# Slot sums of a gathered attention as accumulating float32 transposes, on one Trainium2 core

## The chip, the cores and the metric

The kernel runs on one core of a Trainium2 chip. The metric is device microseconds of one execution; the kernel before has a median of 3311.32 us over three runs (3306.66 to 3313.20). The profile is of one further execution, whose own time was 2781.14 us and whose span in the trace is 2779.3 us. The measured runs are thus 530 us longer than the profiled one, and all rows below come from the profiled one.

Engines: PE is the matrix engine (PEld its weight loads), DVE the vector engine, ACT the scalar engine, POOL the engine that here issues the gathers, SP the one that issues plain loads.

## The reference, cut to what matters

A graph network with four layers over 3327 nodes, each with 256 features. About 0.48% of the adjacency matrix is set, some 16 neighbours per node.

```python
x = ...      # (3327, 256) float32
adj = ...    # (3327, 3327) int32, Bernoulli(0.0048)

# layer 0: one attention score per row, projection, layer norm
h = x @ Wt.T + bt
s = leaky_relu(h @ Wa.T + ba)
w = softmax(where(adj > 0, s, NEG), axis=1)
x = layer_norm(x + (w @ h) @ Wp.T + bp)

# layers 1, 2, 3: multi-head attention over the neighbours, then a feed-forward
for L in (1, 2, 3):
    q, k, v = split(layer_norm(x) @ w_qkv)            # 8 heads of 32
    scores = where(adj != 0, q . k * SCALE, -inf)
    out = softmax(scores) @ v                         # (3327, 256)
    x = x + out @ w_proj + b_proj
    x = x + gelu(layer_norm(x) @ w1 + b1) @ w2 + b2
```

## The kernel before

The kernel makes a list of neighbours for every node, sorts the nodes by number of neighbours, and puts them into 26 blocks of 128. A block b has `CAPS[b]` slots (40 for the fullest, 10 for the emptiest, 448 in all): slot s of node p holds its s-th neighbour. In each layer POOL gathers, for each slot of a block, 128 rows of 512 float32 numbers (key and value), four slots to a buffer, ten buffers in a ring.

DVE multiplies keys with the query and sums per head, ACT takes the exponential, DVE multiplies the values with the weights into `vw` (128 nodes x 4 slots x 256). What is left is the sum over slots, for which PE is used:

```python
def values(self, b, s0):
    ...
    if s0 == 0:
        while len(self.po) > 1:
            self.short.pop(0)()
        self.po[b] = ps_o.tile([P, 512], FP, tag="o", ...)        # one PSUM bank, two of them
    ...
    vw = work.tile([P, GS * D], FP, tag="vw", bufs=3, ...)
    nc.vector.tensor_mul(vw..., v, self.wp[b]...)                  # L1361
    for s in range(0, n, 2):
        m = min(2, n - s) * D
        nc.tensor.matmul(self.po[b][:, :m], ident, vw[:, s * D:s * D + m],   # L1366
                         start=(s0 + s == 0), stop=(s0 + s + 2 >= S), skip_group_check=True)
    self.issue()                                                   # the next gathers of the ring
    if s0 + GS >= S:
        self.short += self.block(b)
```

`ident` is the identity, so a product only copies `vw` into PSUM and adds. Two slots go into one product, so the even and odd slots are summed apart, 256 columns each. The end of a block folds the two, turns the sum (nodes on partitions) into its transpose (features on partitions), which the projection needs as stationary operand, and projects:

```python
def copy():      c["o"] = ...; nc.scalar.copy(c["o"], self.po[b][:, :D])             # L1384
def fold():      nc.vector.tensor_add(c["o"], c["o"], self.po[b][:, D:])             # L1387
def turn():      # two 128x128 transposes back into po                               # L1391
def copy_T():    c["oT"] = ...; nc.scalar.copy(c["oT"], self.po[b][:, :2 * P])       # L1396
def project():   # bias (L1400), then oT @ w_proj into po[:, D:]                     # L1402
def add():       # x += po[:, D:] (L1406), statistics; at the end of a chunk of four blocks
                 # its feed-forward steps are put on the list self.long
return [lambda: None, copy, lambda: None, fold, turn, copy_T, project, lambda: None, add]
```

These short steps are taken one or two at a time between the groups of the blocks that follow, and so are the long steps of a chunk: feed-forward up (L1445) and down (L1468), and the queries, keys and values of the next layer (L1498). Layer 3 has no next layer; it scatters rows of the output instead (L1511).

Ahead of the layers lies a front end that reads the adjacency matrix, makes the lists, and does layer 0. There each group of four blocks counts how many nodes have which number of neighbours. PE adds one-hot rows into `places`, and DVE reads the result:

```python
def soft(self):
    ...
    nc.vector.tensor_tensor(OH[...], num..., top..., ALU.is_equal)          # L892
    at = places[...]
    for j in range(n): ...                                                  # L903
        nc.tensor.matmul(at[:, j, :], lhsT, OH[:, m, :], start=False, stop=True, ...)
    t = aw.tile([P, 4, nd], FP, tag="place", bufs=1, ...)
    nc.vector.tensor_mul(t, at[:, :n, :], OH[:, b0:b0 + n, :])              # L906
    nc.vector.tensor_reduce(rank[:, b0:b0 + n], t, AX.X, ALU.add)           # L907
    if b0 + n == NB:
        ...                                                                 # L909
    # ... small vector work, then two exponentials on ACT
def mix(self): ...                     # the step after: weights times sums
```

Each engine runs its instructions in the order in which the program states them.

Of the kernel before, what the change touches and what calls it, by code (L numbers as in the profile page):

```python
# [8 lines left out]
FP = mybir.dt.float32  # L9
# [3 lines left out]
ALU = mybir.AluOpType  # L13
AX = mybir.AxisListType
# [3 lines left out]
P = 128  # L18
N = 3327
D = 256  # L20
# [12 lines left out]
NB = (N + P - 1) // P  # L33
# [490 lines left out]
def sparse_path(ctx, tc, ins, out, dram, flag):  # L524
    nc = tc.nc
# [97 lines left out]
    with tc.tile_pool(name="a", bufs=1) as a, tc.tile_pool(name="aw", bufs=2) as aw, \  # L623
# [44 lines left out]
        o = 0  # L668
# [172 lines left out]
        class Group:  # L841
# [36 lines left out]
            def soft(self):  # L878


                g, n, b0 = self.g, self.n, self.blocks[0]

                def sv(name):
                    t = aw.tile([P, 4], FP, tag="s_" + name, bufs=1, name=f"s_{name}_{g}")
                    return t[:, :n]

                sg = S.s[:, b0:b0 + n]
                dg = deg[:, b0:b0 + n]
                nc.vector.tensor_copy(dg, self.acc[:, :n, H0])
                top = sv("top")  # L890
                nc.vector.tensor_scalar(top, dg, float(LMAX), None, ALU.min)
                nc.vector.tensor_tensor(OH[:, b0:b0 + n, :],  # L892
                                        num[:, None, :nd].to_broadcast([P, n, nd]),
                                        top[:, :, None].to_broadcast([P, n, nd]), ALU.is_equal)

                at = places[:, :4 * nd].rearrange("p (b k) -> p b k", k=nd)
                for j in range(n):
                    i = b0 + j
                    add = [(tri, i)] + [(ones_bf, k) for k in range(b0, i)]
                    if g:  # L900
                        add += [(rest_tri, i - 4)] + [(ones_bf, k) for k in range(i - 3, b0)]
                    for lhsT, m in add:
                        nc.tensor.matmul(at[:, j, :], lhsT, OH[:, m, :], start=False, stop=True,  # L903
                                         skip_group_check=True)
                t = aw.tile([P, 4, nd], FP, tag="place", bufs=1, name=f"place_{g}")[:, :n]
                nc.vector.tensor_mul(t, at[:, :n, :], OH[:, b0:b0 + n, :])  # L906
                nc.vector.tensor_reduce(rank[:, b0:b0 + n], t, AX.X, ALU.add)  # L907
                if b0 + n == NB:
                    nc.tensor.matmul(at[:, n - 1, :], rest_tri, OH[:, NB - 1, :], start=False,  # L909
                                     stop=True, skip_group_check=True)  # L910
                    S.all = at[:, n - 1, :]
                non, ga, fa, m1, m0, tt, mx = (
                    sv(k) for k in ("non", "ga", "fa", "m1", "m0", "tt", "mx"))
                nc.vector.tensor_scalar(non, dg, -1.0, float(N), ALU.mult, ALU.add)
                nc.vector.tensor_scalar(ga, dg, 0.0, None, ALU.is_gt)
                nc.vector.tensor_scalar(fa, non, 0.0, None, ALU.is_gt)
                nc.vector.tensor_scalar(tt, ga, -NEG0, NEG0, ALU.mult, ALU.add)
                nc.vector.tensor_mul(m1, sg, ga)
                nc.vector.tensor_add(m1, m1, tt)
                nc.vector.tensor_scalar(tt, fa, -1.0, 1.0, ALU.mult, ALU.add)  # L920
                nc.vector.tensor_mul(m0, sg, tt)
                nc.vector.scalar_tensor_tensor(m0, fa, NEG0, m0, ALU.mult, ALU.add)
                nc.vector.tensor_max(mx, m1, m0)
                nc.vector.tensor_sub(m1, m1, mx)
                nc.vector.tensor_sub(m0, m0, mx)
                nc.scalar.activation(m1, m1, AF.Exp)
                nc.scalar.activation(m0, m0, AF.Exp)
                self.non, self.m1, self.m0, self.tt = non, m1, m0, tt

            def mix(self):  # L930
                g, n, b0, acc = self.g, self.n, self.blocks[0], self.acc
                m1, m0, tt = self.m1, self.m0, self.tt
                z = aw.tile([P, 4], FP, tag="s_z", bufs=1, name=f"s_z_{g}")[:, :n]
                nc.vector.tensor_mul(z, deg[:, b0:b0 + n], m1)
                nc.vector.tensor_mul(tt, self.non, m0)
                nc.vector.tensor_add(z, z, tt)
                nc.vector.reciprocal(z, z)
                nc.vector.tensor_mul(m1, m1, z)
                nc.vector.tensor_mul(m0, m0, z)
                shape = [P, n, H0]  # L940
                nb = self.nb = aw.tile([P, 4, H0], FP, tag="nb", bufs=1, name=f"s_nb_{g}")[:, :n]
                t3 = aw.tile([P, 4, H0], FP, tag="t3", bufs=1, name=f"s_t3_{g}")[:, :n]
                nc.vector.tensor_sub(t3, S.hsum[:, None, :].to_broadcast(shape), acc[:, :n, :H0])
                nc.vector.tensor_mul(t3, t3, m0[:, :, None].to_broadcast(shape))
                nc.vector.tensor_mul(nb, acc[:, :n, :H0], m1[:, :, None].to_broadcast(shape))
                nc.vector.tensor_add(nb, nb, t3)

            def project(self):
                g, n = self.g, self.n
# [322 lines left out]
    class Layer:  # L1272
# [77 lines left out]
        def values(self, b, s0):  # L1350

            L, S = self.L, CAPS[b]
            n = min(GS, S - s0)
            t = self.tiles.pop((b, s0))
# [3 lines that stand above are left out]
                self.po[b] = ps_o.tile([P, 512], FP, tag="o", name=f"po_{L}_{b}")  # L1358
            v = t[:, :n, D:2 * D].rearrange("p s (h d) -> p s h d", d=HD)
            vw = work.tile([P, GS * D], FP, tag="vw", bufs=3, name=f"vw_{L}_{b}_{s0}")  # L1360
            nc.vector.tensor_mul(  # L1361
                vw[:, :n * D].rearrange("p (s h d) -> p s h d", h=HEADS, d=HD), v,
                self.wp[b][:, s0:s0 + n, :, None].to_broadcast([P, n, HEADS, HD]))
            for s in range(0, n, 2):
                m = min(2, n - s) * D
                nc.tensor.matmul(self.po[b][:, :m], ident, vw[:, s * D:s * D + m],  # L1366
                                 start=(s0 + s == 0), stop=(s0 + s + 2 >= S),
                                 skip_group_check=True)
            self.issue()
            if s0 + GS >= S:  # L1370
                self.short += self.block(b)


        def block(self, b):
            L, w, c = self.L, self.w, {}
            x = t2[:, b, :D]
            chunk = CHUNK[b]
            if b == chunk[0]:
                self.n2 = Norm(len(chunk), f"f{L}_{b}")
            n2 = self.n2  # L1380

            def copy():
                c["o"] = work.tile([P, D], FP, tag="o", name=f"o_{L}_{b}")
                nc.scalar.copy(c["o"], self.po[b][:, :D])  # L1384

            def fold():
                nc.vector.tensor_add(c["o"], c["o"], self.po[b][:, D:])  # L1387

            def turn():
                for k in range(2):  # L1390
                    nc.tensor.transpose(self.po[b][:, k * P:(k + 1) * P],  # L1391
                                        c["o"][:, k * P:(k + 1) * P], ident)

            def copy_T():
                c["oT"] = work.tile([P, 2 * P], FP, tag="oT", name=f"oT_{L}_{b}")
                nc.scalar.copy(c["oT"], self.po[b][:, :2 * P])  # L1396

            def project():
                ps = self.po[b][:, D:]
                nc.tensor.matmul(ps, ones_bf[:96, :], bias3[:, 0, :], start=True, stop=False)  # L1400
                for k in range(2):
                    nc.tensor.matmul(ps, c["oT"][:, k * P:(k + 1) * P], w["w_proj"][:, k, :],  # L1402
                                     start=False, stop=(k == 1))

            def add():
                nc.vector.tensor_add(x, x, self.po.pop(b)[:, D:])  # L1406
                n2.stats(chunk.index(b), x)
                if b == chunk[-1]:
                    self.long += self.chunk(chunk, n2)
                    at = ORDER.index(b) + 1  # L1410
                    turns = sum(len(slots[i]) for i in ORDER[at:at + CB])
                    turns = 5 if at == NB - 1 else turns - 2
                    self.rate = sum(cost for cost, _ in self.long) / max(turns, 1)

            return [lambda: None, copy, lambda: None, fold, turn, copy_T, project, lambda: None, add]

        def chunk(self, blocks, n2):
            L, w, nxt = self.L, self.w, self.nxt
# [221 lines left out]
```

## Time and profile before

| what | value |
|---|---|
| measured time, median of 3 | 3311.32 us |
| profiled execution, span | 2779.3 us |
| PE busy | 1952.0 us, 70% |
| DVE busy | 1961.9 us, 71% |
| ACT busy | 806.5 us, 29% |
| POOL busy | 1361.8 us, 49% |
| moved by DMA | 453.66 MB, mean 163 GB/s |
| granted PE clock, mean | 0.836 of full |

How to read it: a busy share is an average over the whole span. A row of a group of instructions gives its line, engine and operation, what it writes and reads, its shapes and count, then busy us and mean ns of one, then the idle time of its engine just before it, and what ended most of that. A line of the list of waits gives who waited for whom, the total in us, how many times, and the longest. Slices are fortieths of the span, 69.5 us each, in tenths of busy time. Busy times of PE overlap where matmuls are pipelined, so the spacing of their starts says more than their mean duration. A float32 product shows as two PE records.

### The profile page before, as it was taken

To read this page: it belongs to the slowest core of one execution; us is meant where nothing else is said; L and a number is where in the kernel's file an instruction comes from. 1 tells how busy PE (TensorE), PEld (TensorE's weight loads), DVE (VectorE), ACT (ScalarE), POOL (GpSimd) and SP (SyncE) were. 2 spreads that over 40 slices of the span, in tenths; PEclk is the share of its full clock that TensorE was granted. 3 is DMA by queue.
4 is the path that set the end of the run, shared out by engine and by line. 5 is a ranking of instruction groups with operands and counts; after the bars stand their busy time and mean duration, and the time that the engine had idled before them with its cause. 6 is when DMAs were issued, how large, how long until landed. Compare 5 with 4: busy or idle time off the path is not lost. (4 is left out here: it accounts for less than half of the span.)

```text
span 2779.3 us, 21889 instructions
## 1 busy us (share of the span) xinstructions
PE 1952.0 (70%) x6409; PEld 1045.3 (38%) x6409; DVE 1961.9 (71%) x4061; ACT 806.5 (29%) x1398; POOL 1361.8 (49%) x1458
## 2 busy tenths in 40 slices
PE   5657665248788887884377887887853678867866
PEld 4546553114333333442133443433431333333334
DVE  6597888577877777733788677778427878778852
ACT  5346552102332322321022332232320222222221
POOL 4000000377766666601776565566017777776741
PEclk9768776678899898897788898898976898988988
DMA  6224420677766666613776565566227766666650
GB/s 235 99 106 154 155 81 32 198 217 217 222 196 200 202 182 186 182 34 100 209 211 201 168 195 180 158 190 178 50 70 210 210 183 199 201 190 184 198 130 15
DMA packets 144478, 453.66 MB, mean 163 GB/s; under 512 B 29521, under 2 KB 40156, under 8 KB 141021
## 3 DMA queue, kind: packets, MB, share of 16 engines
q0 software_dynamic: 113056, 370.26, 46.0%
q1 hardware_dynamic: 9834, 53.90, 5.5%
q10 hardware_dynamic: 21458, 28.02, 2.9%
q8 instruction: 52, 0.85, 0.1%
q14 instruction: 78, 0.64, 0.1%
HBM read 420.64 MB, written 31.42 MB: 163 GB/s over the span
## 5 line engine op out<-in xcount | busy, mean ns | idle before, releaser
L1298 POOL DMA_INDIRECT kv<-kv,t x1344 | 1272.8, 947 | 810.0 <-issue 350.4
L1366 PE MATMUL po<-vw,s_ident 128*128 128x512 f32 (+1 forms) x1380 | 770.4, 694 | 497.4 <-DVE vw L1361 447.6
L1320 DVE TENSOR_TENSOR kv<-kv,q 128x1024 f32<-128x1024 f32 (+3 forms) x363 | 413.3, 1139 | 312.6 <-ACT q L1306 156.5
L1366 PEld LDWEIGHTS po<-vw,s_ident 128*128 128x128 f32 x1380 | 285.3, 220 | 846.5 <-issue 468.3
L1321 DVE TENSOR_REDUCE sc<-kv 128x32 f32<-128x1024 f32 (+3 forms) x363 | 414.1, 1141 | 12.4
L1361 DVE TENSOR_TENSOR vw<-kv,w 128x1024 f32<-128x1024 f32 x333 | 371.3, 1127 | 0.2
L1445 PE MATMUL pu<-fT,s_w 128*128 128x512 f32 (+3 forms) x768 | 308.1, 536 | 1.0 <-ACT fT L596 1.0
L1468 PE MATMUL py<-gT,s_w 128*128 128x512 f32 (+2 forms) x672 | 283.4, 549 | 0.0
L1451 ACT ACTIVATE gT<-pu,pvb 128x512 f32<-128x512 f32 (+3 forms) x192 | 116.4, 607 | 361.0 <-PE pu L1445 360.7
L1445 PEld LDWEIGHTS pu<-fT,s_w 128*128 128x128 f32 x768 | 150.6, 206 | 140.5 <-issue 116.0
L711 POOL MEMSET s_abf<- 128x1 bf16 x23 | 2.2, 105 | 375.2 <-DVE s_v L731 248.3
L1468 PEld LDWEIGHTS py<-gT,s_w 128*128 128x128 f32 x672 | 127.6, 191 | 122.0 <-issue 104.4
L723 PE MATMUL s_ptb<-s_ident_bf,s_abf 128*128 128x128 bf16 x676 | 69.8, 273 | 77.3 <-ACT s_abf L714 64.0
L735 DVE MAX8 cand<-s_v 128x8 f32<-128x208 bf16 x416 | 118.0, 359 | 0.9
L588 ACT ACTIVATE xn_f<-t,nm_f,rqy_f 128x256 f32<-128x256 f32 x78 | 42.9, 593 | 247.5 <-DVE nm_f L582 240.1
L1498 PE MATMUL pk<-s_w_qkv,nT 128*128 128x512 f32 x208 | 104.4, 626 | 8.9 <-ACT nT L596 8.9
L1335 ACT ACTIVATE sc<-sc,mx 128x120 f32<-128x120 f32 (+6 forms) x78 | 32.0, 410 | 259.8 <-DVE mx L1332 259.2
L1406 DVE TENSOR_TENSOR t<-t,po 128x256 f32<-128x256 f32 x78 | 32.5, 417 | 103.8 <-PE po L1402 97.9
L1486 DVE TENSOR_TENSOR t<-t,pd 128x256 f32<-128x256 f32 x75 | 29.5, 408 | 91.0 <-PE pd L1482 91.0
L723 PEld LDWEIGHTS <-s_abf 128*128 128x128 bf16 x676 | 58.8, 125 | 91.8 <-ACT s_abf L714 70.8
L855 PE MATMUL s_pa<-s_aT,s_hs 128*128 128x256 bf16 x338 | 80.4, 286 | 13.2 <-DVE s_hs L817 13.2
L724 ACT COPY s_aT<-s_ptb 128x896 bf16<-128x896 bf16 x104 | 82.7, 859 | 19.9 <-PE s_ptb L723 19.7
(292 smaller groups left out, 2343.5 us busy)
## 6 DMA issues: line engine op xcount, KB each, us to landing
s_a<-in_adj_dram SPq DMA_DIRECT2D x25, 1663.5 KB
kv<-kv,t POOLq DMA_INDIRECT x1344, 3.7
kv<-kvr ACTq DMA_DIRECT2D x52, 256.0 KB
kv<-s_kvr ACTq DMA_DIRECT2D x26, 256.0 KB
s_w<-in_L_gnn_w_dram SPq DMA_DIRECT2D x6, 1024.0 KB
t<-ql ACTq DMA_DIRECT2D x6, 592.0 KB
t<-s_x ACTq DMA_DIRECT2D x6, 512.0 KB
s_w_qkv<-in_L_gnn_w_qkv_dram SPq DMA_DIRECT2D x3, 768.0 KB
```

The source lines that it names most:

```text
L723: nc.tensor.transpose(pt[:, m, :], self.abf[:, k * P:(k + 1) * P], ident_bf)
L724: nc.scalar.copy(aT[:, k0:k0 + len(ks), :], pt[:, :len(ks), :])
L735: nc.vector.max(out=self.cand[:, s, :], in_=self.v[:, s, :])
L1298: nc.gpsimd.indirect_dma_start(out=t[:, s, :], out_offset=None, in_=kv[L], in_offset=bass.IndirectOffsetOnAxis(ap=t2[:, b, k:k + 1].bitcas ...
L1320: nc.vector.tensor_mul(k, k, self.q[b][:, None, :].to_broadcast([P, n, D]))
L1321: nc.vector.tensor_reduce(self.sc[b][:, s0:s0 + n, :], k.rearrange("p s (h d) -> p s h d", d=HD), AX.X, ALU.add)
L1361: nc.vector.tensor_mul(vw[:, :n * D].rearrange("p (s h d) -> p s h d", h=HEADS, d=HD), v, self.wp[b][:, s0:s0 + n, :, None].to_broadcast([ ...
L1366: nc.tensor.matmul(self.po[b][:, :m], ident, vw[:, s * D:s * D + m], start=(s0 + s == 0), stop=(s0 + s + 2 >= S), skip_group_check=True)
L1445: nc.tensor.matmul(c["pu", f][:, :n], w["w1"][:, e, f * P:(f + 1) * P], c["hT"][:, e, :n], start=(e == 0), stop=(e == 1))
L1451: nc.scalar.activation(g[:, :n], c.pop(("pu", f))[:, :n], AF.Gelu_apprx_tanh, bias=w["b1"][:, f:f + 1])
L1468: nc.tensor.matmul(c["py"][e][:, :n], w["w2"][:, f, e * P:(e + 1) * P], g[:, :n], start=(f == 0), stop=last)
L1498: nc.tensor.matmul(ps[:, :c1 - c0], c["hT"][:, e, j * P:(j + 1) * P], nxt["w_qkv"][:, e, c0:c1], start=(e == 0), stop=(e == 1))
```

## The change

The product with the identity becomes a transpose that accumulates in PSUM. For each slot PE takes the two halves of `vw` (128 nodes x 128 features) as stationary operand and passes the identity through in transpose mode; the result, 128 features x 128 nodes, is added to what PSUM holds. So the sum over slots comes out transposed as the projection wants it, even and odd slots are not kept apart, and the end of a block needs no copy, fold and turn. The aim is to spare PE the arithmetic of the float32 products, and the other engines the steps at the end of a block.

Apart from that, the front end's reading of `places` moves from `soft` to the end of `mix`, one step of its plan later, so that DVE need not stand and wait for PE there.

```diff
-                t = aw.tile([P, 4, nd], FP, tag="place", bufs=1, name=f"place_{g}")[:, :n]
-                nc.vector.tensor_mul(t, at[:, :n, :], OH[:, b0:b0 + n, :])
-                nc.vector.tensor_reduce(rank[:, b0:b0 + n], t, AX.X, ALU.add)
-                if b0 + n == NB: ...            # (cut: moved along unchanged)
+            def place(self):
+                g, n, b0 = self.g, self.n, self.blocks[0]
+                at = places[:, :4 * nd].rearrange("p (b k) -> p b k", k=nd)
+                t = aw.tile([P, 4, nd], FP, tag="place", bufs=1, name=f"place_{g}")[:, :n]
+                nc.vector.tensor_mul(t, at[:, :n, :], OH[:, b0:b0 + n, :])
+                nc.vector.tensor_reduce(rank[:, b0:b0 + n], t, AX.X, ALU.add)
+                if b0 + n == NB: ...
@@ mix
                 nc.vector.tensor_add(nb, nb, t3)
+                self.place()
@@ values
-            for s in range(0, n, 2):
-                m = min(2, n - s) * D
-                nc.tensor.matmul(self.po[b][:, :m], ident, vw[:, s * D:s * D + m],
-                                 start=(s0 + s == 0), stop=(s0 + s + 2 >= S),
-                                 skip_group_check=True)
+            for s in range(n):
+                for k in range(2):
+                    at = s * D + k * P
+                    nc.tensor.matmul(self.po[b][:, k * P:(k + 1) * P], vw[:, at:at + P], ident,
+                                     is_transpose=True, start=(s0 + s == 0 and k == 0),
+                                     stop=(s0 + s + 1 == S), skip_group_check=True)
@@ block
-            def copy(): ...
-            def fold(): ...
-            def turn(): ...
-            return [lambda: None, copy, lambda: None, fold, turn, copy_T, project, lambda: None, add]
+            return [lambda: None, copy_T, project, lambda: None, add]
```

More of the change, by code (lines that the diff above doesn't have):

```diff
@@ L904, in soft @@
                                          skip_group_check=True)
-                t = aw.tile([P, 4, nd], FP, tag="place", bufs=1, name=f"place_{g}")[:, :n]
-                nc.vector.tensor_mul(t, at[:, :n, :], OH[:, b0:b0 + n, :])
-                nc.vector.tensor_reduce(rank[:, b0:b0 + n], t, AX.X, ALU.add)
[L908 to L911, printed above, removed]
                 non, ga, fa, m1, m0, tt, mx = (
@@ L928, in soft @@
                 self.non, self.m1, self.m0, self.tt = non, m1, m0, tt
+            def place(self):
[4 more added lines that the diff above has]
+                nc.vector.tensor_reduce(rank[:, b0:b0 + n], t, AX.X, ALU.add)
+                if b0 + n == NB:
+                    nc.tensor.matmul(at[:, n - 1, :], rest_tri, OH[:, NB - 1, :], start=False,
+                                     stop=True, skip_group_check=True)
+                    S.all = at[:, n - 1, :]
             def mix(self):
@@ L1380, in block @@
             n2 = self.n2
[L1382 to L1392, printed above, removed]
             def copy_T():
```

## The prediction

> **What bounds the kernel now.** I read the page's first two parts, then its costliest groups, then busy time in 30 us stretches, then the waits, and last the chain of work that ended last.
>
> Page, busy shares and the 40 slices:
>
> ```profile
> PE 1952.0 (70%) x6409; PEld 1045.3 (38%) x6409; DVE 1961.9 (71%) x4061; ACT 806.5 (29%) x1398; POOL 1361.8 (49%) x1458
> ...
> PE   5657665248788887884377887887853678867866
> DVE  6597888577877777733788677778427878778852
> ...
> POOL 4000000377766666601776565566017777776741
> PEclk9768776678899898897788898898976898988988
> ```
>
> No engine is full. POOL separates five parts: a front end without gathers (to 521 us, the first gather), and three layers of gathers, each followed by a tail in which POOL is at 0 or 1 (the next layer cannot gather before the last row of keys and values is written).
>
> Costliest groups:
>
> ```profile
> L1298 POOL DMA_INDIRECT kv<-kv,t x1344 | 1272.8, 947 | 810.0 <-issue 350.4
> L1366 PE MATMUL po<-vw,s_ident 128*128 128x512 f32 (+1 forms) x1380 | 770.4, 694 | 497.4 <-DVE vw L1361 447.6
> L1320 DVE TENSOR_TENSOR kv<-kv,q 128x1024 f32<-128x1024 f32 (+3 forms) x363 | 413.3, 1139 | 312.6 <-ACT q L1306 156.5
> ```
>
> The slot sums are PE's largest item, 770 of 1952 us. POOL's timeline shows 0.30 us between gathers of 0.95 us: one per 1.25 us at best. Layer 1 issues 473 POOL transfers between 521.1 and 1179.7 us (447 gathers of keys and values, 26 of rows): 473 x 1.25 = 591 of 659 us, so 67 us of stall. Layer 2: 448 in 649 us, 560, stall 89. Layer 3: 467 in 609 us (some are output rows), 584, stall 25. Together 181 us. The stalls come once per chunk of four blocks, about every 103 us in layers 1 and 2.
>
> Who is late when POOL stalls? Two short stretches of layer 1, then one whole period of layer 2 and a stretch of layer 3:
>
> ```profile
> core 0: us, PE busy (x) PEld busy (x) DVE busy (x) ACT busy (x) POOL busy (x), PEclk, DMA share, GB/s
> ...
> 950.00:980.00 30.00, 30.00 (x71) 13.73 (x70) 21.43 (x32) 10.72 (x21) 20.37 (x22) 0.92 0.68 195
> 1160.00:1190.00 30.00, 30.00 (x76) 13.73 (x76) 16.88 (x18) 9.63 (x22) 15.81 (x17) 1.00 0.72 165
> ...
> 1702.00:1804.00 102.00, 83.58 (x215) 39.29 (x214) 76.18 (x133) 30.62 (x52) 60.99 (x65) 0.88 0.59 175
> ...
> 2450.00:2540.00 90.00, 70.22 (x174) 31.99 (x173) 69.31 (x108) 22.43 (x35) 64.96 (x69) 0.89 0.66 196
> ```
>
> Columns: stretch, length, busy time of PE, PE weight loads, DVE, ACT, POOL, granted clock, DMA. PE is busy for the whole of the first two at nearly full clock, while DVE is at 71 and 56% and POOL issues 22 and 17 transfers where 24 would fit. A period of layer 2 holds 65 transfers, 81 us at POOL's best, but takes 102, with PE busy for 84 and DVE for 76. Layer 3 gets 69 into 90 us. It has the same slot sums but no projection of the next layer (line 1498, 104 + 53 us for two layers), and it stalls 25 us instead of 89. So PE is what makes layers 1 and 2 late, in bursts. DVE itself waits behind it; its list of waits in layer 1 begins:
>
> ```profile
> DVE kv L1320 <- ACT q L1306: 62.9, 14, 7.2
> DVE t L1406 <- PE po L1402: 33.4, 10, 6.5
> ```
>
> ACT is late there because its queue stands at a copy out of PSUM that PE has not filled (the waits list ACT for 117.5 us behind line 1366 and 124.4 behind line 1391, in all).
>
> **What the skill says.** "Perfetto Trace Analysis", in Optimizing Tensor Performance, Transposes: a transpose should be issued as one, since it skips the arithmetic. The chain that ended last has both side by side at one clock:
>
> ```profile
> 2709.93 0.45 PE pd L1482 x4
> ...
> 2713.01 3.62 PE po L1366 x4
> ...
> 2717.06 1.72 PE po L1366 x4
> ```
>
> Four float32 transposes take 0.45 us, 0.11 each; four passes of the slot product take 1.72, 0.43 each, or 3.62 at half clock. "FP8 and Floating Point Precision", TensorE Precision Notes, says a true float32 product needs four passes. The trace agrees: each product is two records, and each streams 512 columns in 0.43 us, 0.84 ns a column, against 0.11 us for 256 bf16 columns in line 855: four times as long in all. A float32 transpose is one record of 128 columns at the same 0.84 ns. "PSUM — Partial Sum Buffer", The four PSUM rules, says a float32 transpose sets the bits as a matmul does, so it should accumulate; no run here shows it yet. "TensorE: Matmul & The Clock Gate", Part 4, warns that transposes don't count as activity for the clock. This trace disagrees, for bf16: the 3.4 us from 105.1 us hold 26 transposes and no other matmul at a granted clock of 0.50, and the next 3.4 us have 0.99.
>
> **The change, part by part.**
>
> *Slot sums.* Four slots were two products of 512 columns, four records, 4 x 0.43 = 1.72 us at full clock. They become eight transposes, 8 x 0.11 = 0.88 us; each has its own weight load, but in the transposes of line 591 loads and passes overlap (starts 0.21 us apart at half clock, 0.11 at full). So 0.84 us less per four slots, or 0.21 per slot; 1344 slots give 282 us at full clock, some 330 at the granted mean of 0.836. At half clock a group falls from 3.4 to 1.7 us. The order of PE's instructions keeps one wait on DVE per group, so no wait is added.
>
> *Block end.* Copy, fold and two transposes go, 78 times: ACT 78 x 0.37 = 29 us, DVE 78 x 0.41 = 32 us, PE 156 x 0.11 = 17 us, and one of two ACT stops behind PE for each block. The chain from last sum to projection loses 0.38 + 0.43 + 0.45, with gaps about 1.3 us.
>
> *Count of places.* In the front end DVE reads the counts right after PE was asked for them:
>
> ```profile
> DVE place L906 <- PE places L903: 41.1, 7, 16.2
> ```
>
> Seven waits, 41 us, up to 16, nearly all of DVE's idle time between 110 and 470 us, where it is about 86% busy. Read at the end of the next step, the wait should be over by then; work is unchanged.
>
> Sum for the path, stage by stage:
> - Front end: 41 us of waits on its fullest engine; I take 35.
> - Layers: if PE's 89 and 67 us of stalls fell to layer 3's 25, 106 us would go, and 10 in layer 3. But a period of layer 2 then has 74 us of DVE work in some 84, 88%, and DVE waits in order for others; so I take 100 of the 181.
> - Three tails: each holds ten groups of slot sums (40 records of line 1366 between 1190 and 1300 us, 23.9 us busy). Where PE is full they give 0.84 us each, 8.4, and the block end 1.3: 10. In the last tail six records more run at half clock, so 13. Together 33.
>
> That is 168 us of the profiled 2779. The measured time, 3311 us, is 532 longer than the profiled execution, and nothing in the profile says where those lie. Carried over one for one it gives 3143; in proportion (x 1.19), 3111. I choose 3130.
>
> **Rivals.**
> 1. *Gathers are the bound, and more so without the profiler.* For: POOL is already at its best spacing in the first 200 us of every layer and the gathers are the natural place for another 0.4 us each (532 / 1344). Then layers have few stalls for PE to cause, and only front end and tails gain, 35 + 33 plus a little: about 3230. Against: in the profile the stalls follow PE.
> 2. *DVE takes over.* For: per four slots it does 3 x 1.2 us, and a period of layer 2 has 76 us of DVE work. Then layers gain only some 50 us: 3190. Against: its waits are mostly behind ACT and PE, which shrink.
> 3. *The clock falls.* Less work on PE, and in a form that the skill says is not counted, means more half-clock stretches, and the feed-forward products pay. The feed-forward is 590 us of busy time (lines 1445 and 1468); at a mean clock of 0.70 in place of 0.84 it takes 118 more, and with that much of the layers' gain goes: about 3220. Against: the bf16 transposes above.
> 4. *The extra 532 us are PE at half clock.* Then halving its slot sums is worth about double: 3000.
>
> **Range and chances.** The centre is 3130; the rivals lie at 3230, 3190, 3220 and 3000. Range 3030 to 3225. Faster by over 2% is below 3245, which even the first three reach: 0.88. Within 2%: 0.10. Slower would need transposes that don't stream when they accumulate: 0.02.
>
> **What would show it.** The row of slot sums should have 2688 records with a mean near 300 ns and 350 to 420 us busy. The wait of DVE for the places should be under 5 us and the first gather near 486 us. POOL's stalls in layers 1 and 2 should fall to about 25 us each, the silent stretches between layers from 123 to about 112 us, and the granted clock stay above 0.75. I am wrong if the transposes start more than 0.15 us apart at full clock, if the stalls stay and end on DVE, or if the profiled gain does not appear in the measured time.

## The result, and the profile after

The changed kernel took 3142.61 us (median of four runs, 3125.22 to 3158.07) beside 3310.58 us for the kernel before: a ratio of 0.9492, 95% interval [0.9441, 0.9543]. That is within 13 us of the predicted 3130. The way there was not the predicted one, and a good part of this text is about that.

First the page of the changed kernel, an execution of 3158.07 us (span 3156.3): busy shares, the 40 slices, and three groups of instructions (busy us and mean ns of one, then the idle time of the engine ahead of them and what ended most of it).

```profile
PE 1794.0 (57%) x7561; PEld 1163.5 (37%) x7561; DVE 1935.3 (61%) x3983; ACT 774.6 (25%) x1316; POOL 1362.7 (43%) x1458
...
PE   4767752255666666671457667666713435665556
...
POOL 4000004545555554305555555544054555565550
PEclk9868766577787886785578778878755766776768
...
L1372 PE MATMUL po<-s_ident,vw 128*128 128x128 f32 x2688 | 475.4, 334 | 580.2 <-DVE vw L1366 387.2
...
L1400 DVE TENSOR_TENSOR t<-t,po 128x256 f32<-128x256 f32 x78 | 32.6, 418 | 390.8 <-remote 254.5
L1445 ACT ACTIVATE gT<-pu,pvb 128x512 f32<-128x512 f32 (+3 forms) x192 | 115.7, 607 | 628.2 <-remote 384.1
```

The slot sums are there as predicted, 2688 records in place of 1380, 475 us busy in place of 770. But PE is busy for 158 us less in a span that is 377 us longer than the profiled span of before, and POOL's slices, 6 and 7 in the layers of before, are 5 and 4. The new thing is the word "remote" at the end of two rows: ACT and DVE were released by something whose origin the profile does not find among the recorded instructions. Both wait there for PE. (Engines tell each other of finished work by counting up semaphores; one such step is called an increment here.) The list of waits of the same execution has three of these rows among its first ten:

```profile
ACT gT L1445 <- remote: 384.1, 31, 29.6
...
ACT oT L1390 <- remote: 320.2, 21, 40.8
...
DVE t L1400 <- remote: 254.5, 16, 24.0
```

One such moment, 24 us of layer 1 cut in three (stretch, length, then busy us of PE, PE weight loads, DVE, ACT, POOL, the granted clock, DMA):

```profile
736.00:743.30 7.30, 4.95 (x16) 2.75 (x16) 1.71 (x5) 0.75 (x2) 5.47 (x7) 1.00 0.78 218
743.30:752.60 9.30, 0.00 (x0) 0.00 (x0) 0.00 (x0) 0.00 (x0) 4.50 (x5) 0.62 0.64 182
752.60:760.00 7.40, 6.01 (x17) 4.32 (x18) 6.65 (x8) 2.31 (x7) 4.11 (x5) 0.56 0.54 147
```

PE's last matmul before the pause, a product of the next layer's queries, ends at 743.27 by the records. Then PE, DVE and ACT do nothing at all for 9.3 us, until an increment of PE's count arrives at 752.69 and DVE starts the product `vw` that had waited for it. From 753.47 seven more increments come within 0.31 us. So other engines learnt over 9 us late of what PE had finished by the records. The ends of matmuls in the profile are modelled, though; whether PE finished late or was only heard of late, this does not tell. Of the 1105 recorded increments by PE some 190 come over 0.2 us after the end of any recorded matmul, up to 24.5 us after. In the profile of before there are 3, all after 2772 us, at the program's very end, and the others come within about 15 ns.

That profile is thus of another condition than the profile of before, and the two can't be laid on each other. The experiments give the pair that can: the kernels ran on four chips, called A to D here, and the kernel before took 2780 us on A and C, but 3275 and 3297 us on B and D. Every profile taken on B and D has the late increments (some 160 to 210 of them); those of A and C have 3 each, at the end. Each chip was used at one time only, so chip and time can't be told apart here; "on B" is short for both.

The changed kernel on chip C, 2570.04 us (span 2567.3), the same rows of its page:

```profile
PE 1675.1 (65%) x7561; PEld 1122.4 (44%) x7561; DVE 1939.4 (76%) x3983; ACT 780.4 (30%) x1316; POOL 1362.1 (53%) x1458
...
PE   5658775426588677874367778787723765775676
...
POOL 4000000177777777712777767666047767776770
PEclk9778777657788788887577889788865877877888
...
L1303 POOL DMA_INDIRECT kv<-kv,t x1344 | 1273.4, 947 | 643.4 <-issue 327.7
L1372 PE MATMUL po<-s_ident,vw 128*128 128x128 f32 x2688 | 454.6, 328 | 499.8 <-DVE vw L1366 498.4
...
L1325 DVE TENSOR_TENSOR kv<-kv,q 128x1024 f32<-128x1024 f32 (+3 forms) x363 | 413.5, 1139 | 282.5 <-DMA kv<-kv,t 172.3
```

This is what was expected: POOL at 7 where it was 6 and 7, PE down to 65%, DVE the fullest engine with 76%. PE's idle time ahead of the slot sums is now all but 1.4 us a wait for DVE, and DVE's own row says what it waits for most: no longer ACT standing behind PE, as in before, but the gathered rows. That is a sum over stages, however, and 112 of the 172 us lie in layer 3; in layers 1 and 2 DVE still waits longer behind ACT (43 us in each) than for rows (29 and 27). Layer 2 as one stretch (the columns are those above) has DVE busy for 480.54 of 587.6 us, 82%, and PE for 406.07, 69%; the kernel before had 75% of both in the 651.7 us that it took on chip A:

```profile
1201.10:1788.70 587.60, 406.07 (x1608) 258.08 (x1608) 480.54 (x781) 161.44 (x269) 423.68 (x447) 0.79 0.72 207
```

### The profile page after: what moved, and what is told of

It is laid out like the page before. It is cut to its first block, busy times and chain, and to the rows that moved or that the text cites. A ratio compares the mean times of both kernels' runs of the same rounds, so it can differ in the third digit from the quotient of the medians.

```text
span 3156.3 us, 24036 instructions
## 1 busy us (share of the span) xinstructions
PE 1794.0 (57%) x7561; PEld 1163.5 (37%) x7561; DVE 1935.3 (61%) x3983; ACT 774.6 (25%) x1316; POOL 1362.7 (43%) x1458
## 4 chain that ended last, share of the span: by engine, by line
DVE 25%; issue 18%; PE 18%; another core or an unknown queue 17%; POOL 11%; ACT 5%; DMA 5%; DVEq 0%; ACTq 0%; POOLq 0%; SPq 0%
POOL kv L1303 11%; DVE kv L1325 5%; DMA kv<-kv,t 4%; DVE sc L1326 3%; DVE vw L1366 3%; PE pu L1439 3%; PE po L1372 3%; PE py L1462 2%; DVE cand L735 2%; PE pk L1492 1%; PE s_pk L1010 1%; ACT s_aT L724 1%; DVE s_v L731 1%; PE pf L591 1%
## 5 line engine op out<-in xcount | busy, mean ns | idle before, releaser
L1372 PE MATMUL po<-s_ident,vw 128*128 128x128 f32 x2688 | 475.4, 334 | 580.2 <-DVE vw L1366 387.2
L1372 PEld LDWEIGHTS po<-s_ident,vw 128*128 128x128 f32 x2688 | 395.5, 174 | 724.1 <-issue 373.5
L1439 PE MATMUL pu<-fT,s_w 128*128 128x512 f32 (+3 forms) x768 | 341.2, 579 | 62.3 <-issue 35.8
L1462 PE MATMUL py<-gT,s_w 128*128 128x512 f32 (+2 forms) x672 | 321.8, 597 | 58.1 <-issue 50.2
L1439 PEld LDWEIGHTS pu<-fT,s_w 128*128 128x128 f32 x768 | 157.4, 222 | 196.1 <-issue 146.4
L1396 PEld LDWEIGHTS po<-s_w_proj,oT 128*128 128x128 f32 x312 | 71.8, 255 | 281.8 <-issue 272.3
L1394 PE MATMUL po<-bias,s_ones_bf 96*128 96x256 bf16 x78 | 25.2, 324 | 259.7 <-issue 147.4
L1390 ACT COPY oT<-po 128x256 f32<-128x256 f32 x78 | 28.9, 371 | 548.5 <-remote 320.2
L1492 PE MATMUL pk<-s_w_qkv,nT 128*128 128x512 f32 x208 | 128.4, 748 | 22.0 <-ACT nT L596 9.9
L1396 PE MATMUL po<-s_w_proj,oT 128*128 128x256 f32 x312 | 113.1, 500 | 0.0
L591 PE MATMUL pf<-s_ident,xn_f 128*128 128x128 f32 x156 | 46.1, 444 | 86.8 <-ACT xn_f L588 66.7
```

Source lines behind the costliest of these rows:

```text
L1372: nc.tensor.matmul(self.po[b][:, k * P:(k + 1) * P], vw[:, at:at + P], ident, is_transpose=True, start=(s0 + s == 0 and k == 0), stop=(s0 ...
L1439: nc.tensor.matmul(c["pu", f][:, :n], w["w1"][:, e, f * P:(f + 1) * P], c["hT"][:, e, :n], start=(e == 0), stop=(e == 1))
L1462: nc.tensor.matmul(c["py"][e][:, :n], w["w2"][:, f, e * P:(e + 1) * P], g[:, :n], start=(f == 0), stop=last)
L1492: nc.tensor.matmul(ps[:, :c1 - c0], c["hT"][:, e, j * P:(j + 1) * P], nxt["w_qkv"][:, e, c0:c1], start=(e == 0), stop=(e == 1))
```

## The experiments

Stages are read from POOL's gathers as in the prediction: first to last transfer of a layer, minus 1.25 us for each step from one to the next, is its stall; from the last transfer of a layer to the first of the next is a silent stretch (the third is the last tail).

| kernel, chip | front end to | stalls L1, L2, L3 | silent stretches | median us | ratio to before, 95% |
|---|---|---|---|---|---|
| before, A | 515.6 | 69, 93, 26 | 126, 121, 96 | 2777.96 | 0.9990 [0.9978, 1.0001] |
| places only, A | 501.2 | 72, 87, 26 | 126, 121, 96 | 2762.30 | 0.9925 [0.9897, 0.9952] |
| sums only, A | 516.4 | 13, 32, 28 | 98, 98, 66 | 2586.21 | 0.9302 [0.9271, 0.9333] |
| changed, half the transposes, A | 501.7 | 5, 16, 27 | 96, 95, 68 | 2540.45 | 0.9137 [0.9106, 0.9168] |
| changed, C | 498.9 | 13, 29, 29 | 98, 98, 69 | 2570.04 | 0.9237 [0.9212, 0.9262] |
| changed, list of nine, C | 498.9 | 37, 57, 25 | 115, 112, 90 | 2669.65 | 0.9598 [0.9574, 0.9621] |
| changed, B | 505.4 | 203, 201, 162 | 116, 118, 82 | 3129.99 | 0.9551 [0.9491, 0.9610] |
| changed, list of nine, B | 508.8 | 233, 236, 189 | 137, 137, 106 | 3275.38 | 0.9990 [0.9968, 1.0012] |
| products for transposes, B | 506.8 | 251, 220, 196 | 132, 133, 97 | 3264.62 | 0.9981 [0.9952, 1.0009] |
| long list over 8 turns, B | 503.6 | 201, 200, 166 | 116, 118, 82 | 3133.08 | 0.9557 [0.9514, 0.9600] |
| products for transposes, D | 506.9 | 252, 231, 192 | 135, 132, 92 | 3280.53 | 0.9897 [0.9871, 0.9924], of 9 of its 20 runs |
| changed, list of three, D | 505.0 | 252, 243, 188 | 104, 106, 94 | 3228.25 | 0.9788 [0.9743, 0.9834] |

Ratios are to the kernel before on the same chip: 2779.73 (A), 3274.57 (B), 2781.62 (C), 3297.42 us (D).

### The parts of the change, on chip A

The kernel before, unchanged:

> The kernel before, unchanged. The earlier profile of it spans 2779 us while its measured runs take 3310. Theory A: the measured runs spend the difference inside the span, in PE work that completes late in the layers, as the profile of the changed kernel shows (191 PE completions later than 0.2 us after the last recorded matmul); then this run takes 3310 +- 15 us, its profile spans about as much, the front end is as in the earlier profile (first gather near 520 us), and the layers are some 500 us longer, with late PE completions. Theory B: the 530 us lie outside the span; then the profile is again near 2779 us with completions on time. Ratio to before 1.00 in both.

It took 2777.96 us. Both theories had missed: the measured run is neither 530 us longer than its profile nor 3310. The 530 us that the prediction could not place are not something that the profiler hides in each run; they belong to the condition in which the first comparison ran.

Only the later reading of the count of places, slot sums as before:

```diff
 def soft(self): ...
-    t = ...; tensor_mul(t, at, OH); tensor_reduce(rank, t)     # L906, L907
 def mix(self): ...
+    self.place()                                               # the same, a step later
```

> The kernel before with only the reading of the counts of places moved from soft to the end of mix; slot sums stay identity products. By the prediction's sum, 35 us less: 3275. By what the first gather of the changed kernel says (504 us against 520 in the earlier profile of before), 15 us less: 3295. The first gather tells which.

It took 2762.30 us, 21 us less by the ratio (interval 13 to 29) and 17 by the medians, of which 14.4 are seen before the first gather: nearer to the 15 than to the 35 us. DVE's list of waits in its front end shows where the rest of the 38.7 us that it waited for the places has gone:

```profile
DVE s_z L938 <- ACT s_m L919: 7.6, 2, 4.4
DVE s_x L986 <- ACT s_x L980: 7.2, 2, 5.8
DVE s_x L972 <- PE s_pp L963: 6.8, 3, 5.0
DVE deg L889 <- ACT s_acc L876: 5.6, 1, 5.6
DVE place L927 <- PE places L903: 5.3, 2, 2.7
```

The wait fell to 5.3 us. But in before's list the first and third of these rows do not stand at all and `s_x <- ACT` (line 981 there) has 5.8: DVE came earlier to results of ACT and PE that were no earlier, and 16 of the 33 us came back as waits for these.

Only the slot sums as transposes, with the shorter block end; the places as before:

```diff
-    nc.tensor.matmul(po[b][:, :m], ident, vw[:, s*D:s*D+m], ...)
+    nc.tensor.matmul(po[b][:, k*P:(k+1)*P], vw[:, at:at+P], ident, is_transpose=True, ...)
-    return [nil, copy, nil, fold, turn, copy_T, project, nil, add]
+    return [nil, copy_T, project, nil, add]
```

> The changed kernel with the counts of places read in soft as before: only the slot sums and the end of a block are changed. Theory (halved PE work in the layers and tails): most of the gain is here, 3310 - 150 = 3160 us, with the first gather back near 520 us. Rival (the gain comes mostly from the front end, as rival 1 of the prediction had it): 3250 or more.

2586.21 us: 194 us for this part alone, so the gain is not one of the front end. The places and the sums add up, 21 + 194 = 215, to what the whole change gives on C, 1 - 0.9237 or 212 us.

The changed kernel with the second transpose of each slot left out after a block's first slot. The sums of the upper 128 features then hold the first slot only; PE does 1422 of the 2688 transposes:

```diff
-    for k in range(2):
+    for k in range(2 if s0 + s == 0 else 1):
```

> The changed kernel, but after the first slot of a block only the first of the two transposes of each slot is issued: features 128 to 255 of the attention are not summed over the slots, so half of the slot-sum work of PE is left out. If PE's work in the slot sums still sets the pace in the layers, as much again goes as half of what the change spared: about 75 us less than the changed kernel, 3065. If the gathers or DVE set it now, less than 25 us: 3120 or more.

2540.45 us, a ratio of 0.9137 against 0.9237 for the whole change on C, some 28 us. That is nearer to the 25 us of the second theory than to the 75 of the first. PE's remaining time for the sums is not free, but 1266 transposes of 0.11 us are 139 us at full clock, and only a fifth of that is on the path. The stalls of layers 1 and 2 go down to 5 and 16. Layer 3's stays at 27.

### What is in the 194 us: halved sums, or a shorter list

Four runs on chip B, where the kernel before took 3274.57 us. The changed kernel again:

> The changed kernel once more, beside the kernel before. Theory A (the 5% of the first comparison was measured where PE's completions come late; where they come on time the change is worth more): if before takes some 2780 us here, this takes 2568 (the sums alone took 2586, the places 15 to 17 less), ratio 0.924; if before takes some 3310 here, this takes 3140 again and the late completions are back in its trace. Theory B (the late completions belong to the changed program): 3140 even where before takes 2780.

3129.99 us, 0.9551, as in the first comparison, and some 190 late increments are in its trace. So the change is worth 5% where increments come late. How much where they don't, this run can't say.

The same operands multiplied in place of transposed, so that only the form of the PE instruction is as in before (two records of 128 columns for each half of a slot, 5376 in all):

```diff
-    is_transpose=True, start=(s0 + s == 0 and k == 0), ...
+    start=(s0 + s == 0 and k == 0), ...
```

> As the changed kernel, but the slot sums are true float32 products of the same operands in place of transposes: po transposed, no copy, fold and turn, 5 steps per block, two records of 128 columns per half. Theory A (most of the gain is the halved PE time of the sums): four slots take 1.7 us again, the stalls of layers 1 and 2 stay above 55 us each, and only places and the shorter block end gain: 2700 us against 2780, ratio 0.97. Theory B (most of the gain is the shorter block end, with fewer stops of ACT and DVE): at most 2620, ratio 0.945 or less.

3264.62 us: nothing gained, 0.9981, which is neither theory. And the transposes with four empty entries put back into the short list. No work is added; only the projection, and what is put on the long list after it, is called as many turns after the block's last sum as in before:

```diff
-    return [nil, copy_T, project, nil, add]
+    return [nil, nil, nil, nil, nil, copy_T, project, nil, add]
```

> As the changed kernel, but the list of short steps of a block again has nine entries, the four additional ones empty: same work, the projection and what follows on it only start as many turns after the block's last sum as in the kernel before. Theory A (the tails lost 28, 23 and 30 us, not 33 together, because the shorter list leaves less feed-forward for after the last gather): the silent stretches grow by 10 to 15 us each over the changed kernel's and the PE records of line 1462 in the first tail rise from 32 toward 52: 2600 us. Theory B (it is the work of copy, fold and turn that is gone, or PE's shorter sums alone): same as the changed kernel within 0.3%.

3275.38 us: nothing gained either, 0.9990. On this chip the change is worth its 145 us only with both parts, for which no cause was found. I had expected 30 us of the list, and neither theory had this.

> As the changed kernel, but the feed-forward of the last chunk but one is spread over 8 turns in place of 5. Theory A (PE is the bound in the first 60 us of a tail, and block 0's sums stand in its queue behind that feed-forward): each silent stretch falls by 5 to 10 us, 2550 us. Theory B (the tail is set by the total of PE's work in it): no difference, or up to 10 us longer each.

```diff
-    turns = 5 if at == NB - 1 else turns - 2
+    turns = 8 if at == NB - 1 else turns - 2
```

3133.08 us, the same as the changed kernel within the scatter, and the silent stretches are equal to 0.7 us. How that long list is spread over turns does not matter there.

The list of nine and the changed kernel were then run on chip C, where the kernel before took 2781.62 us:

> The nine steps with empty entries again, to see it where before takes some 2780 us. Theory A: on such a run the longer list costs only the tails, 25 to 35 us: 2600 us, ratio 0.935; the 145 us that it cost where before takes 3275 came with late completions of PE. Theory B: the longer list costs the same 145 us anywhere: 2715, ratio 0.977. If before takes some 3300 us here, the ratio is 0.999 again.

> The changed kernel beside it. Theory A: where before takes some 2780 us this takes 2568, ratio 0.924, with the stalls of layers 1 and 2 at some 13 and 30 us and silent stretches of 98, 98 and 66 us. Theory B (the change is worth 5% anywhere): 2640, ratio 0.95. If before takes some 3300 us here: 3130, ratio 0.955.

2669.65 and 2570.04 us. The changed kernel gives 0.9237 [0.9212, 0.9262], as expected; the list of nine was between the two theories. Four empty entries cost 100 us, nearly half of what the change is worth, although PE and DVE run as many instructions as without them (7561 and 3983). The trace shows what they move. PE works in the order of the program (the 7561 records of the changed kernel come in the same order on B and C, however long it waits), so one can count how many of the slot sums stand ahead of a chunk's first feed-forward product (L1439; 8 records are a group of four slots, a layer has 112 groups). In layer 1 it is 14.2, 30.0, 46.5 ... 95.8 groups with five entries and 18.8, 35.0, 51.2 ... 102.0 with nine. Every chunk of feed-forward comes some 5 groups later, the last but one 6. The ring holds ten groups, so ten are left when the last gather has been issued. With nine entries the feed-forward of the last chunk but one begins just when only these ten are left (102 of 112). With five it begins 16 groups from the end.

It shows in the rows of PE in the first silent stretch, first before (chip A), then the list of nine, then the changed kernel (both chip C):

```profile
L1366 PE MATMUL po<-vw,s_ident 128*128 128x512 f32 x40 | 24.3, 744 | 18.0 <-DVE vw L1361 18.0
L1445 PE MATMUL pu<-fT,s_w 128*128 128x256 f32 (+2 forms) x73 | 18.2, 385 | 0.3 <-ACT fT L596 0.3
L1468 PE MATMUL py<-gT,s_w 128*128 128x256 f32 (+1 forms) x52 | 17.3, 461 | 0.0
```

```profile
L1440 PE MATMUL pu<-fT,s_w 128*128 128x256 f32 (+2 forms) x74 | 19.1, 393 | 0.5 <-ACT fT L596 0.3 <-ACT gT L1446 0.2
...
L1463 PE MATMUL py<-gT,s_w 128*128 128x256 f32 (+1 forms) x52 | 17.3, 461 | 0.0
L1372 PE MATMUL po<-s_ident,vw 128*128 128x128 f32 x80 | 12.1, 304 | 17.1 <-DVE vw L1366 17.1
```

```profile
L1439 PE MATMUL pu<-fT,s_w 128*128 128x256 f32 (+1 forms) x64 | 15.5, 384 | 0.9 <-ACT fT L596 0.9
L1372 PE MATMUL po<-s_ident,vw 128*128 128x128 f32 x80 | 11.1, 295 | 0.0
L1462 PE MATMUL py<-gT,s_w 128*128 128x256 f32 x32 | 7.9, 379 | 0.0
```

The ten groups of sums take 24.3 us in the first and 12.1 and 11.1 in the others: this is the halving. The feed-forward of the stretch, 73 + 52 records in before, is 74 + 52 with the list of nine and 64 + 32 with the list of five: 13 us of PE's work were done before the last gather. The first silent stretch is 125.8, 114.6 and 97.7 us long.

That is the tail. In the layers the list shows in DVE's wait for the projection, which the step `add` reads. In layer 1 it is, before (A), with the list of nine and with the list of five (both C):

```profile
DVE t L1406 <- PE po L1402: 36.2, 11, 6.5
```

```profile
DVE t L1400 <- PE po L1396: 34.3, 14, 5.7
```

```profile
DVE t L1400 <- PE po L1396: 14.5, 8, 4.8
```

In layer 2 it is 40.1, 35.7 and 14.9. So about 20 of the 24 and 28 us of stall that the four entries cost in these layers are DVE standing behind PE at this step. There are as many turns between `project` and `add` in both lists; why DVE finds the projection done more often with the short one is not shown.

So on A and C: with the list of nine kept, the transposes, the missing copy, fold and turn, and the places give 112 us (17 of them in the front end); the list of five gives 100 more. How much of the 112 is the halved PE time and how much the missing copy, fold and turn is told in part by the traces. In the first tail the 11 us less are about the 12 us less of PE's ten groups. In layer 2, which is 36 us shorter with the list of nine than before, DVE works 6.6 us less and waits 4.7 us less for a copied sum to fold, which is the missing block end; it also waits 17 us less behind ACT, to which both may have led. The products were to tell more:

> The products in place of the transposes again (shorter list, no copy, fold and turn, places moved, but PE's time for the sums as before), to see it where before takes some 2780 us. Of the 210 us that the change gives there, the shorter list was shown to be worth 100 with PE's time halved. Theory A (halved PE time and shorter list each count for themselves): the list's 100 plus the places' 15 and some 10 of removed work go, 2655 us, ratio 0.955, stalls of layers 1 and 2 near 35 and 60 us. Theory B (each helps only with the other, as where before takes 3275): 2740 or more, ratio 0.985. If before takes some 3300 us here, the ratio is 0.998 again.

But this was on chip D, with 3297.42 us for the kernel before, and gave 3280.53. By the medians of all runs that is 0.995, as on chip B (0.997); the 0.9897 of the table counts only the nine runs within 1.5% of a single fastest one, 3229.88 us, although the other eleven have the same granted clock. What the shorter block end gives without the halving where increments are on time has not been measured.

A list of three, with both empty entries gone:

```diff
-    return [nil, copy_T, project, nil, add]
+    return [copy_T, project, add]
```

> As the changed kernel, but the two empty entries of the short list are gone too: three steps per block, the copy right after the block's last sum. Theory A (what counts is how early the projection and its feed-forward come into the queues; five entries in place of nine gave 100 us): another 20 to 50 us less, 2530 us, and less feed-forward in the tails. Theory B (the empty entries let ACT come to its copy after PE has finished the sum; without them ACT stands behind PE): 10 to 30 us more, 2590 us. Where before takes some 3300 us: 3130 less or more by the same.

3228.25 us, 0.9788, where the changed kernel had 0.9551 on chip B and 0.9492 in the first comparison; it was not run on D. The silent stretches of layers 1 and 2 are shorter than on B by 12 and 11 us, as theory A has it, but that of layer 3 is longer by 12, and the stalls are longer by 49, 42 and 25. That would fit theory B, ACT standing at its copy behind PE, but it is another chip and the late increments are in it; on chips A and C the list of three was not run, so neither theory is shown. No other kernel that computes everything came below the changed kernel's ratio on any chip where both were run.

## Why the prediction was right, and where it was not

**The number.** The sum was 168 us, carried over one for one to 3143, and the measured difference is 168.0 us. That is a coincidence of two things: on runs without late increments the change gives 212 us, more than the sum, and with them some of it is lost. 3143 lies in the stated range all the same; the sentence that led to it, that 532 us of unknown kind simply stay, was not what happened. Where they sit can be seen in full only for the changed kernel, B against C: layer stalls 203 + 201 + 162 against 13 + 29 + 29, silent stretches 18, 19 and 13 us longer, the front end 6.5 us. PE busy is 1789.8 against 1675.1 us, and PE is at half clock for 1653 us against 1111.

**Slot sums, 1.72 to 0.88 us per group: right.** In the chain that ended last of the changed kernel on C a group in the first silent stretch reads

```profile
1143.40 0.87 PE po L1372 x8
```

so accumulating transposes stream just like plain ones (and they do add: 20 to 80 of them go into one block's sum). The starts of the 2688 transposes are 0.100 to 0.115 us apart in 1453 cases and 0.205 to 0.220, half clock, in 723. The row's busy time, foreseen as 350 to 420 us, is 455 on C and 475 in the first comparison, and the mean 328 and 334 ns, not 300: with the sums halved, PE waits longer for DVE ahead of them (498 us against 448), and more of them start at half clock.

**Front end, 35 of 41 us: oversized.** 17 us on C, 14 for the places alone on A. The wait itself went as foreseen (38.7 to 5.3). The step that failed is "nearly all of DVE's idle time ... Read at the end of the next step, the wait should be over": it counted the wait removed as time removed, and did not ask for what DVE would stand next.

**Layers, 100 of 181 us: right in size, in parts for another reason.** Stalls on A and C went from 69 and 93 to 13 and 29 us, together 120 less. With the list of nine they are 37 and 57, which is 68 less; the other 52 are the list. The floor of 25 us was taken from layer 3, and this was wrong, as was the 10 us expected there. Layer 3's stall is no stall of PE. POOL's list of waits in layer 3 has, before (A) and changed (C):

```profile
POOL out_dram L1511 <- DMA out_dram<-t,perm: 14.6, 6, 3.8
```

```profile
POOL out_dram L1505 <- DMA out_dram<-t,perm: 28.1, 10, 7.2
```

POOL waits there for its own transfers of output rows. For the changed kernel these 28.1 us are nearly all of the 29 us of stall, in before 14.6 of 26, with DVE ending most of the rest (10.5). The stall of 25 to 29 us stayed in every kernel on A and C. For layer 2 the same lists show what did go (POOL waits there for DVE to be done with a buffer, and DVE stands behind PE and ACT):

```profile
POOL kv L1298 <- DVE vw L1361: 100.3, 27, 10.0
```

```profile
POOL kv L1303 <- DVE vw L1366: 35.4, 25, 3.1
```

**Three tails, 33 us: this is the step that failed.** The silent stretches fell by 28, 23 and 27 us, 78 in all. "They give 0.84 us each, 8.4, and the block end 1.3: 10" was well worked out for what it counted: with the list of nine the three fell by 11, 9 and 7, 27 us. What it left out is that the diff also makes a list of nine entries into one of five. The prediction quoted the list and priced its entries by their durations, as 29 us of ACT, 32 of DVE and 1.3 of chain; the place that an entry gives to all that follows was not counted, and that was worth 100 us: 50 in the tails and some 50 in the layers. The wait that it shortened in the layers was among the lines that the prediction showed (`DVE t L1406 <- PE po L1402: 33.4`), without a price.

**The rivals.** Rival 1, gathers that are slower in themselves by 0.4 us, is out: the median spacing of gathers is 1.254 us on B and 1.251 on C. What grew are the pauses, spacings of over 2 us: 126 with 997 us together against 54 with 378, the first two silent stretches among them. Rival 2, DVE takes over: it is the fullest engine now, and PE waits for it (498 us ahead of the slot sums), but in layers 1 and 2 it waits itself, behind ACT and for gathered rows. The layers gained more than the 50 us of this rival; whether DVE took a part of what more could have been gained, no run tells. Rival 3, the clock: its mean fell from 0.83 to 0.784 on C and 0.735 on B, as half-clock stretches became more (947 us on A before, 1111 on C); but the layers on C are 116 us shorter than on A before in sum all the same. Rival 4, the 532 us as half-clock time, is out as stated, though PE is at half clock for nearly all of the additional time: what it does there is stand idle. Its busy time differs by 115 us between B and C, the time by 560, the half-clock time by 542.

**What would show it.** Records of the sums, 2688: yes. Wait for the places under 5: 5.3 to 6.5. First gather near 486: 498.9 to 505. Stalls near 25: 13 and 29 on C, some 200 on B. Silent stretches near 112: 98 on C, 116 and 118 on B. Clock above 0.75: 0.784 on C, 0.735 on B. Of the three ways to be wrong none came: transposes are 0.11 us apart, the stalls that are left in layer 2 end on DVE but are 29 us where they were 93, and the profiled gain appears in the measured time, where both are of one chip.

## What to carry to other kernels

In a kernel that hands out its steps from lists, turn by turn, count a changed list by where it puts the work behind it in the queue of the bound engine, not only by the durations of the entries: four empty entries cost 100 us here. When a wait on a full engine is taken away, ask what that engine waits for next, and take the lower bound of a stall from a stage only after reading which wait ends it there. And before a measured time is laid beside a profile, see that both are of one condition; a difference of 19% between them was the loudest line in this case, and it was a difference of the chip or the hour.

## What was not expected of the hardware

**Late increments.** On two chips of four, PE's increments of semaphores reach ACT and DVE late, in the changed kernel on B up to 23 us after the last matmul that the trace has, while those of DVE (median 11 to 12 ns after the end) and ACT (9 ns) come at once. It begins with the gathers: before the first of them there are 6 of over 1 us, at most 2, in that run. The increments then come in bursts, eight within 0.4 us at 753.5 us, and PE stands idle meanwhile. Its time in pauses of over 8 us after 500 us is 496 us on B against 194 on C. PE itself is held up too, not only its messages: on B 65 matmuls that wait for no semaphore start after 0.3 to 2.5 us of idle PE, 72 us in all, and with the products in place of the transposes 188, 212 us in all; on A and C there is none.

Gathers run in these pauses (the DMA share is 0.64 in the one shown), but an end of the gathers isn't what frees the increments: some come with all 16 DMA engines busy, as at 1305.1 us of that run after 10 us of waiting. The number of PE's records doesn't decide: the products, with a third more of them, have 631 us of lateness in sum over their late increments on B, the changed kernel 870, and the list of nine, with the same PE instructions in another order, 1868. Fewer increments are recorded too, of every engine: PE 1109 on B against 1258 on C, DVE 2502 against 3136, ACT 926 against 1162, with the same instructions recorded. So single ones can't always be told, and that the recording itself holds the engines up there is a rival that no run tests. Why it is so was not found. No trace of the kernel before was taken on B or D, so what a stage of it loses there is open as well.

**Transposes and the clock.** In the changed kernel on C there are 15 stretches of 3.4 us after the front end at a granted clock of 0.50 with at least 12 float32 transposes and no other matmul. The next 3.4 us have 1.00 in 12 of them. (The stretches are those of the grid on which the granted clock changes.) Of the 161 stretches of this kind with fewer than 12 such transposes, or with nothing on PE, only 1 is followed by full clock. So here the transposes themselves raised the clock. "TensorE: Matmul & The Clock Gate" of the Trainium skill, Part 4, says that full clock doesn't engage for transposes, since they do not count as busy time in the same way; the prediction found that this does not hold for bf16 here, and the same goes for float32.
